# A two-layer graph network on one core: ScalarE's queue reordered, gate sums in two buffers, filter matrices loaded one by one

## The chip, the cores and the metric

One core of one Trainium2 chip. The time is the device time of one execution in microseconds; each kernel is executed several times, on the same chip in turn with the kernel before, and the median is quoted. A ratio is the mean time of one kernel's fast runs over the mean of the other's fast runs of the same rounds, so it is not quite the ratio of the medians quoted beside it. A profile adds one traced execution; its span is about 2 us shorter than the device time.

Engines are named as in the profile: PE is TensorE (PEld its weight loads), DVE VectorE, ACT ScalarE, POOL GpSimd, SP SyncE, which issues most transfers (415 of the 514 in the profile of the kernel before).

## The reference, cut to what matters

For 64 graphs ("items") of 256 nodes with 256 features, in float32:

```python
# layer 0
h      = relu(bn1(conv1x1(x^T)))
x_conv = relu(bn2(conv17(h)) + x^T)^T                  # 17 taps along the nodes
s      = x @ w_se.T + b_se                             # 3 numbers per node
A      = exp(-dist(s, s)) * adj
x_nmp  = A @ relu(x @ w_msg.T + b_msg)
gi     = [x_conv, x_nmp] @ w_ih.T + b_ih;  gh = x @ w_hh.T + b_hh
r, z   = sigmoid(gi_r + gh_r), sigmoid(gi_z + gh_z)
n      = tanh(gi_n + r * gh_n)
x      = layernorm(x + (1 - z) * n + z * x)
# layer 1
h      = layernorm(x)
x      = layernorm(x + relu(adj @ h @ W_rel + b_rel + h @ W_root))
```

## The kernel before

The gates of one item are three sources (`nmp`, `x`, `xc`) times a 2 x 2 block matrix. The kernel uses a Strassen-like scheme with seven block products instead of eight; "U5" is the product with index 4, which goes into the bank `b_`, is copied to `g11`, and whose bank is then used again by the product with index 2. All matmul outputs of this kernel rotate through eight PSUM banks (`bufs=8`), so a bank that was not read in time holds up whichever matmul comes eight banks later (in the kernel before, ps_b waited 85.5 us in all for the copy of U5).

```python
def gates(k):
    g = work.tile([P, C, 2, HG], F32, name="g", bufs=1)
    ...
    block_product(k, 0, a, True);   nc.scalar.copy(g00, a[:, :HG])
    block_product(k, 1, d, True);   ve.tensor_add(g00, g00, d[:, :HG])
    nc.gpsimd.tensor_add(g00, g00, bg[:, 1, :])
    yield
    block_product(k, 4, b_, True);  nc.scalar.copy(g11, b_[:, :HG])      # the copy of U5, L710
    block_product(k, 6, c_, True);  ve.tensor_add(g11, g11, c_[:, :HG])
    yield
    block_product(k, 5, a, False)
    ve.tensor_add(<g01 and g10>, <a twice>, bg)
    nc.gpsimd.tensor_add(g11, g11, g01)
    yield
    block_product(k, 2, b_, False); ve.tensor_add(g01, g01, b_[:, :HG])   # needs the bank b_ read
    nc.scalar.activation(<tanh of g0>)
    yield
    block_product(k, 3, c_, False); ve.tensor_add(g10, g10, c_[:, :HG])
    nc.scalar.activation(<tanh of g1>)
    yield

def update(k):                     # last part of three: layer norm of the item
    ...                            # VectorE: bn_stats; GpSimd: add, pow, mul, scale -> sh, q
    for i, dst in ((1, H[k]), (0, w)):
        for n in range(C):         # h and x1: four ScalarE instructions, L774
            nc.scalar.activation(dst[:, n, :], w[:, n, :], AF.Identity, bias=sh[...], scale=q[...])

def factors(k):                    # transposes st into a bank, ScalarE copies it out twice (lr)
    ...
def aggregate(k):                  # y: four steps; the third is Square on ScalarE, then GpSimd
    ...                            # (scale, pow, mul), the fourth the last Identity on ScalarE
```

In these traces an engine's instructions stand in the order in which the program emits them (moving one emitted step by four lines moved the copy of U5 ahead of h and x1 in 63 of 64 items, see order_only). The program software-pipelines three to four items; the order within the loop over items is therefore the schedule:

```python
for k in range(b * BG, (b + 1) * BG):
    ga, up = gates(k), update(k)
    load(k + 3)
    step(ga)                        # products 0, 1
    step(y_left)                    # y of item k - 2, second step
    step(up_left)                   # h and x1 of item k - 1
    pump()                          # a share of the next block's convolution
    step(ga)                        # products 4 (U5), 6
    mask(k + 1)
    step(y_left)                    # y, third step (Square)
    pump()
    step(ga)                        # product 5
    step(y_left)                    # y, fourth step (waits for GpSimd)
    pump()
    factors(k + 2)                  # lr: two ScalarE copies
    step(ga)                        # product 2
    ...
    transposes_h(k - 1); messages(k + 3); pump()
    passing(k + 1); sums(k + 1, "x")
    step(ga)                        # product 3
    ...
```

`pump()` emits the convolution of the next block of eight items, which is done by an FFT-like transform on VectorE with products on TensorE. It is paced by a fixed estimate of both engines' times, so the mix of VectorE work is decided when the program is built.

## Time and profile before

| | before |
|---|---|
| median time | 2394.8 us (3 runs) |
| TensorE busy | 2173.5 of 2392.4 us |
| VectorE busy | 1869.8 us |
| granted TensorE clock, mean | 0.962 |
| TensorE's waits in all (sum of that view) | 210.3 us |

Read it as two engines near their limit that wait for one another: 219 us of TensorE and 523 us of VectorE are idle. Most of VectorE's idle time lies where it has no transform to do; the stretches in the prediction show the part where both are nearly full. The lines of this profile stand in the prediction.

### The profile page before, as it was taken

The numbers are of one execution on the slowest core, as the hardware profiler recorded it, in microseconds if no ns is written. First come the engines' busy times: TensorE is split into PE (matmuls) and PEld (weight loads), VectorE is DVE, ScalarE is ACT, GpSimd is POOL, SyncE is SP. The second block draws the span as 40 slices with busy tenths as digits, with TensorE's granted clock in tenths as the row PEclk, the third lists the DMA queues.
The fourth block names the chain that finished last, engine by engine and source line by source line (L and its number), as shares of the span: only waits on it lengthen the run. The fifth ranks groups of instructions, "written<-read, shape, count | busy, mean of one in ns | idle before, by whom it ended". The sixth has DMA issues, their size and how long they took to land. (4 is left out here: it accounts for less than half of the span.)

```text
span 2392.4 us, 26243 instructions
## 1 busy us (share of the span) xinstructions
PE 2173.5 (91%) x8390; PEld 1508.2 (63%) x8390; DVE 1869.8 (78%) x4172; ACT 946.0 (40%) x2065; POOL 506.9 (21%) x744
## 2 busy tenths in 40 slices
PE   7878898898989999899988999889998999989996
PEld 4555576665766666666666667666676666766664
DVE  3895899758986699948988489875898669996563
ACT  4414332453235442354323533245323544235443
POOL 1002221222122231122212132122212223112221
PEclk9989999999989999999999999999999999999998
DMA  5533152221522234131432215222152222411110
GB/s 158 183 133 115 31 172 84 84 84 56 173 75 95 69 102 148 55 110 49 139 117 71 97 38 171 85 87 84 53 177 71 94 71 97 153 56 58 45 36 18
DMA packets 213942, 226.80 MB, mean 95 GB/s; under 512 B 22327, under 2 KB 205614, under 8 KB 213806
## 3 DMA queue, kind: packets, MB, share of 16 engines
q1 hardware_dynamic: 191248, 191.14, 24.8%
q10 hardware_dynamic: 22558, 33.99, 3.8%
q8 instruction: 68, 1.11, 0.2%
q14 instruction: 68, 0.56, 0.1%
HBM read 179.22 MB, written 45.88 MB: 94 GB/s over the span
## 5 line engine op out<-in xcount | busy, mean ns | idle before, releaser
L106 DVE SCALAR_TENSOR_TENSOR XF<-XF 128x512 f32<-128x512 f32 (+2 forms) x800 | 521.9, 688 | 6.8
L106 DVE TENSOR_TENSOR XF<-XF 128x256 f32<-128x256 f32 (+3 forms) x480 | 357.5, 764 | 43.9 <-ACT XF L494 36.3
L106 PE MATMUL ps_k<-w,XF 128*128 128x256 f32 x1316 | 295.1, 380 | 2.9 <-DVE msg L106 1.5
L106 PEld LDWEIGHTS ps_k<-w,XF 128*128 128x128 f32 x1316 | 250.8, 191 | 51.4 <-issue 4.3
L106 PE MATMUL ps_out<-wrr,hT 128*128 128x512 f32 x512 | 232.2, 596 | 4.6 <-ACT hT L788 4.6
L106 PE MATMUL ps_b<-wg,nmpsum 128*128 128x384 f32 x256 | 115.5, 535 | 107.7 <-ACT g L710 85.5
L764 POOL TENSOR_TENSOR q<-mv,eps 128x4 f32<-128x4 f32 x64 | 12.9, 202 | 917.8 <-DVE mv L106 917.8
L106 PEld LDWEIGHTS ps_out<-wrr,hT 128*128 128x128 f32 x512 | 97.4, 192 | 103.4 <-issue 89.2
L106 PE MATMUL ps_nmp<-AT,msg 128*128 128x256 f32 x512 | 130.5, 400 | 25.2 <-DVE g L106 22.5
L774 ACT ACTIVATE h<-x,sh,q 128x256 f32<-128x256 f32 x128 | 69.8, 593 | 200.9 <-POOL sh L768 200.9
L631 POOL TENSOR_SCALAR st<-ns 128x4 f32<-128x4 f32 x64 | 25.4, 397 | 580.8 <-DVE sq L106 357.8
L106 DVE TENSOR_TENSOR g<-g,ps_c 128x384 f32<-128x384 f32 x128 | 70.4, 550 | 90.6 <-ACT g L710 63.9
L106 PE MATMUL ps_msg<-wms,xT 128*128 128x260 f32 x512 | 127.8, 393 | 3.9 <-DMA adj<-in_adjT_dram 3.5
L106 PEld LDWEIGHTS ps_b<-wg,nmpsum 128*128 128x128 f32 x256 | 44.2, 198 | 137.6 <-ACT g L710 93.6
L106 PE MATMUL ps_out<-hr,adj 128*128 128x256 f32 x512 | 128.1, 392 | 1.0 <-ACT hr L800 0.9
L106 PEld LDWEIGHTS ps_nmp<-AT,msg 128*128 128x128 f32 x512 | 99.8, 199 | 43.4 <-DVE g L106 25.4
L106 PE MATMUL ps_c<-xTc,w 128*128 128x512 f32 x256 | 118.2, 604 | 8.6 <-ACT xTc L483 8.6
L718 POOL TENSOR_TENSOR g<-g 128x384 f32<-128x384 f32 x64 | 84.5, 1320 | 183.9 <-DVE g L106 183.2
L106 DVE TENSOR_TENSOR msg<-ps_msg,bmsg 128x256 f32<-128x256 f32 x128 | 52.5, 416 | 88.7 <-PE ps_nmp L106 88.7
L106 PE MATMUL ps_n<-wn,xT 128*128 128x256 f32 x512 | 120.9, 379 | 0.0
L106 PE MATMUL ps_c<-wg,nmp 128*128 128x384 f32 x256 | 110.0, 513 | 9.1 <-DVE y L106 9.1
L831 ACT ACTIVATE y<-y,sh,v 128x256 f32<-128x256 f32 x128 | 69.9, 593 | 121.1 <-POOL sh L828 118.3
(144 smaller groups left out, 4442.3 us busy)
## 6 DMA issues: line engine op xcount, KB each, us to landing
w<-w2m SPq DMA_DIRECT2D x105, 768.0 KB, 5.0
xn<-in_x_dram SPq DMA_DIRECT2D x32, 512.0 KB, 4.3
xt<-xTc ACTq DMA_DIRECT2D x32, 512.0 KB, 4.8
xT<-xt SPq DMA_DIRECT2D x64, 256.0 KB, 3.0
adj<-in_adjT_dram SPq DMA_DIRECT2D x64, 256.0 KB, 3.7
x<-in_x_dram SPq DMA_DIRECT2D x64, 256.0 KB, 2.7
xb<-in_x_dram SPq DMA_DIRECT2D x32, 512.0 KB, 3.5
out_dram<-y ACTq DMA_DIRECT2D x64, 256.0 KB, 2.2
```

The costliest lines, as they stand in the source:

```text
L106: return op(o, *args, **kwargs)
L631: nc.gpsimd.tensor_scalar(twice[:, :, :, 3], ns.unsqueeze(2).to_broadcast([P, C, 2]), 0.5, None, ALU.mult)
L718: nc.gpsimd.tensor_add(g11, g11, g01)
L764: nc.gpsimd.tensor_tensor(q, mv[:, :, 1].unsqueeze(1).to_broadcast([P, 2, C]), eps2, ALU.add)
L774: nc.scalar.activation(dst[:, n, :], w[:, n, :], AF.Identity, bias=sh[:, i, n:n + 1], scale=q[:, i, n:n + 1])
L831: nc.scalar.activation(y[:, n, :], y[:, n, :], AF.Identity, bias=sh[:, n:n + 1], scale=var[:, n:n + 1])
```

## The change

Its intent: ScalarE is idle most of the time but is waited for, because ready copies stand behind steps that wait for GpSimd. So the copy of U5 goes ahead of h and x1; the relu of the messages, which waits for VectorE, goes to a later place; g gets a second buffer, so that the first copy of an item need not wait for the last reader of the item before; the sum of g11 is rearranged; the block of the messages (nmp) is multiplied last and its sums are made earlier. The memory for the second g comes from loading the filters one matrix at a time (14 KB in place of 18 KB per partition) and from a single AT.

```diff
 def load_w(b, first, n):
-    t = work.tile([P, 3, C, D], F32, tag="w2", name="w2", bufs=3)
-    nc.sync.dma_start(out=t[:, :n], in_=w2m[first:first + n].rearrange("f c p o -> p f c o"))
-    return lambda m, c: t[:, m, c, :]
+    ts = [work.tile([P, C, D], F32, tag="w2", name="w2", bufs=7) for _ in range(n)]
+    for m, t in enumerate(ts):
+        nc.sync.dma_start(out=t, in_=w2m[first + m].rearrange("c p o -> p c o"))
+    return lambda m, c: ts[m][:, c, :]
 ...
-        nc.scalar.activation(MSG[k], MSG[k], AF.Relu)          # in messages(k)
+    def rectify(k):
+        nc.scalar.activation(MSG[k], MSG[k], AF.Relu)
 ...
-        AT[k] = work.tile([P, C, N], F32, tag="AT", name="AT")
+        AT[k] = work.tile([P, C, N], F32, tag="AT", name="AT", bufs=1)
 ...
-        for j, (name, w) in enumerate((("nmp", ...), ("x", ...), ("xc", ...))):
+        sources = [("xc", ...), ("x", ...), ("nmp", ...)]
+        for j, (name, w) in enumerate(sources if k % BG else sources[::-1]):
 ...
-        g = work.tile([P, C, 2, HG], F32, name="g", bufs=1)
+        g = work.tile([P, C, 2, HG], F32, name="g")            # two buffers
 ...
-        nc.gpsimd.tensor_add(g11, g11, g01)
+        ve.tensor_add(g11, g11, a[:, :HG])
+        nc.gpsimd.tensor_add(g11, g11, bg[:, 0, :])
 ...                                                            # the loop over items
             step(y_left)
-            step(up_left)
             pump()
             step(ga)
             mask(k + 1)
+            step(up_left)
             step(y_left)
 ...
+            sums(k + 1, "x"); sums(k + 1, "xc")                # before passing, not after
             pump()
             passing(k + 1)
 ...
             project(k - 1)
+            sums(k + 1, "nmp")                                 # was after distances
             step(up)
             pump()
             distances(k + 2)
+            rectify(k + 3)
```

(Guards for the last items, and the start before the first item, are cut.)

More of the change, by code (lines that the diff above doesn't have):

```diff
@@ L689, in block_product @@
     def block_product(k, i, ps, start):
-        for j, (name, w) in enumerate((("nmp", wg[:, i, 1, :]), ("x", wx[:, i, :]), ("xc", wg[:, i, 0, :]))):
+        sources = [("xc", wg[:, i, 0, :]), ("x", wx[:, i, :]), ("nmp", wg[:, i, 1, :])]
+        for j, (name, w) in enumerate(sources if k % BG else sources[::-1]):
             te.matmul(ps[:, :w.shape[-1]], LEFT[k, name][i], w, start=start and j == 0, stop=j == 2,
-                             skip_group_check=not start)
+                      skip_group_check=not start)
     def gates(k):
-        g = work.tile([P, C, 2, HG], F32, name="g", bufs=1)
+        g = work.tile([P, C, 2, HG], F32, name="g")
         G[k] = g
@@ L925, in weight_sums @@
                 nc.gpsimd.tensor_sub(w[:, i], w[:, j], w[:, l])
-    early = [lambda: messages(0), lambda: messages(1), lambda: factors(0), lambda: distances(0), lambda: mask(0),
-             lambda: factors(1), lambda: distances(1), lambda: passing(0), lambda: messages(2),
+    early = [lambda: messages(0), lambda: rectify(0), lambda: messages(1), lambda: rectify(1), lambda: factors(0), lambda: distances(0), lambda: mask(0),
+             lambda: factors(1), lambda: distances(1), lambda: passing(0), lambda: messages(2), lambda: rectify(2),
              lambda: sums(0, "x"), lambda: weight_sums((6, 2, 4), (4, 4, 0)), lambda: sums(0, "nmp"),
@@ L976, in gnn_two_layers @@
                 messages(k + 3)
+            if k + 1 < B:
+                sums(k + 1, "x")
+                if (k + 1) % BG:
+                    sums(k + 1, "xc")
             pump()
@@ L979, in gnn_two_layers @@
                 passing(k + 1)
-                sums(k + 1, "x")
             step(ga)
@@ L985, in gnn_two_layers @@
                 project(k - 1)
-            if k + 1 < B and (k + 1) % BG:
-                sums(k + 1, "xc")
+            if k + 1 < B:
+                sums(k + 1, "nmp")
             step(up)
@@ L991, in gnn_two_layers @@
                 distances(k + 2)
-            if k + 1 < B:
-                sums(k + 1, "nmp")
+            if k + 3 < B:
+                rectify(k + 3)
             pump()
```

## The prediction

> **What bounds the kernel now.** I read the page's busy line first, then the busy time in stretches of 14 us, then the waits of TensorE and VectorE, then one stalled item in the timeline. The busy line says TensorE is the busiest engine:
>
> ```profile
> PE 2173.5 (91%) x8390; PEld 1508.2 (63%) x8390; DVE 1869.8 (78%) x4172; ACT 946.0 (40%) x2065; POOL 506.9 (21%) x744
> ```
>
> 2392.4 - 2173.5 = 219 us of TensorE is idle. By 100 us stretches, 52 of it lies in the first 200 us (filters are built, the change does not touch them) and 18 in the last 92; about 149 us lie in the 2100 us between. There the 64 items run in eight blocks of eight, and beside each block but the last VectorE carries the transform of the next block's convolution. The stretches show what that means (columns: the stretch, its length, busy us and count of PE, PEld, DVE, ACT, POOL, then granted clock, DMA share, GB/s):
>
> ```profile
> 1276.00:1290.00 14.00, 10.70 (x40) 7.75 (x39) 11.98 (x29) 7.47 (x18) 6.85 (x10) 0.88 0.21 75
> 1290.00:1304.00 14.00, 14.00 (x51) 8.82 (x50) 13.72 (x32) 3.72 (x9) 0.17 (x1) 1.00 0.28 96
> 1304.00:1318.00 14.00, 10.97 (x44) 8.18 (x43) 8.41 (x17) 8.41 (x18) 6.85 (x10) 0.76 0.27 93
> ```
>
> The first two together are one item: TensorE has 24.7 us of work, VectorE 25.7. Both are nearly full, and both lose about 3 us at the same place. Over a whole transform stretch (1080 to 1318 us) TensorE is busy 217.7 of 238 us and VectorE 210.9. So the kernel has two bounds of almost equal size, and the idle time comes from their waiting for one another and for a third. The waits name the third:
>
> ```profile
> PE ps_b L106 <- ACT g L710: 85.5, 29, 4.1
> PE ps_nmp L106 <- DVE g L106: 22.5, 7, 3.7
> PE ps_b L106 <- DVE nmpsum L106: 22.1, 14, 2.7
> ```
>
> ```profile
> DVE g L106 <- ACT g L710: 63.9, 30, 4.0
> ...
> DVE g L106 <- POOL g L718: 34.4, 34, 1.3
> ...
> DVE XF L106 <- ACT XF L435: 30.2, 21, 3.0
> ```
>
> L710 is ScalarE's copy of the fifth gate product (U5) out of its bank. ScalarE is only 40% busy, so it is late because of its order and not its load. One case:
>
> ```profile
> 1306.42 0.22 POOL L768 TENSOR_SCALAR sh<-sh 128x4 f32<-128x4 f32 x1
> ...
> 1306.68 1.09 ACT L774 ACTIVATE h<-x,sh,q 128x256 f32<-128x256 f32 x2 [3.54 <-POOL sh L768]
> ...
> 1307.67 1.08 ACT L774 ACTIVATE x<-x,sh,q 128x256 f32<-128x256 f32 x2
> 1308.65 0.46 ACT L710 COPY g<-ps_b 128x384 f32<-128x384 f32 x1
> ...
> 1309.14 0.56 DVE L106 TENSOR_TENSOR g<-g,ps_c 128x384 f32<-128x384 f32 x1 [2.86 <-ACT g L710]
> 1309.16 0.50 PEld L106 LDWEIGHTS ps_b<-wg,nmpsum 128*128 128x128 f32 x2 [3.31 <-ACT g L710]
> 1309.16 1.65 PE L106 MATMUL ps_b<-wg,nmpsum 128*128 128x384 f32 x2 [3.03 <-ACT g L710]
> ```
>
> The bank was ready about 1302; the copy stood behind h and x1 of the item before, which stood behind four GpSimd steps of the statistics. One further wait holds the head of that queue:
>
> ```profile
> ACT g L702 <- DVE x L106: 115.1, 35, 8.2
> ```
>
> L702 writes the only buffer of g, which VectorE still reads for the item before.
>
> [...] a ready 0.46 us copy waited for two groups it does not need. [...] Here a 3.03 us wait was followed by a pair of matmuls in 1.65 us that takes 0.81 elsewhere, with a granted clock of 0.76 in that stretch; the 2.84 us wait at 555 us was followed by 0.91. So some stalls cost more than their length. [...]
>
> **The change part by part.**
> Reordering ScalarE: h and x1 (4 x 0.59 us and the wait for the statistics) go behind the copy of U5. The order of the built program confirms it: the sums' two copies now stand next to one another, then h and x1. This removes L710 as a cause: 85.5 us on TensorE, 63.9 us on VectorE. Since VectorE is the tighter one in those items (13.72 of 14 in the second half), I count its 63.9 us and not the 85.5. In the products stages a copy of a filter product (L435) stood behind h and x1 too: at 1231 us VectorE waited 2.97 us for it. Once per block, 7 x 2.9, gives 20 us of the 30.2.
> Two buffers of g: takes away the 115.1 us of L702. By itself this is ScalarE's idle time; it lets L710 come early, so it is in the 63.9 already.
> The sum g11: GpSimd's add of g01 becomes a VectorE add from the bank, 64 x 0.55 us (the row of the same shape from PSUM) = 35.2 us more VectorE work. It removes VectorE's wait for GpSimd before it overwrites g01, 34.4 us. Net +1.
> Order of sums and sources: the nmp block is multiplied last in seven items of eight, so its sums have 1.4 us more (0.81 and 0.59 us of matmuls), and its sums stand earlier on VectorE. That attacks 22.1 us on TensorE; where VectorE is the bound it only moves the wait. I count 5.
> Relu of messages later: its 173.2 us of ScalarE waiting (L629) no longer holds the copy of nmp behind it. Its reader comes two items later. Counted in the 5.
> Filters one by one: 7 buffers of 2 KB per partition in place of 3 of 6, with AT in one buffer (-2 KB): this pays for the second g (+6 KB). It makes 112 transfers into 329 of 256 KB. No TensorE wait for them is in the waits of before; seven matrices lead by one group of six (5.3 us of matmuls) plus the 3.5 us of other work between groups, against some 3 us to land. I count 0.
> Sum: 63.9 + 20 - 1 + 5 = 88 us. As items shorten, other waits grow (VectorE for the messages' product, 88.7 us today; TensorE for VectorE). I take off a quarter: 66 us, so 2394.8 - 66 = 2329 us, 2.8% less.
>
> **The rivals.**
> VectorE takes the place of ScalarE. For: 13.72 of 14 us in the half item after a stall, and 35 us of new work. Against: it idles 27 us of those 238 itself. If only a third of the gain survives, 2394.8 - 30 = 2365.
> TensorE is freed fully. If all of the 149 us but VectorE's share went: a transform stretch can't go under 218 of 238 us, 20 us seven times, 2255. The slow clock after stalls speaks for a part of it; two engines in fixed orders at 91 and 90% speak against the whole.
> A transfer or the later h takes over. The filters' lead falls from nine matrices to seven and SyncE waits 457 us for buffers already. h is wanted by the transposes one gate product after its new place; if they waited 1 us in 64 items, +64 us and the gain is gone. In the trace h is done by 1307.8 where its transposes start at 1314, so moving it 0.5 to 2 us is safe there.
>
> **Range and chances.** The 88 us undiscounted and some better clock give 2298; a discount of 60% gives 2362. The 2% line lies at 2347, 48 us down. My middle of 66 lies 18 us beyond it, with a spread of about 28 us: faster 0.73, within 2% 0.26, slower 0.01.
>
> **What would show it.** Right: the wait of ps_b for L710 (renumbered) falls from 85.5 us to under 10, VectorE's for it likewise; ScalarE's copy of ps_a no longer waits for VectorE's x; VectorE's busy time grows by about 35 us to 1905; the granted clock rises above 0.962; transform stretches show VectorE near 95%. What TensorE then waits for is VectorE. Wrong: a wait of ps_hT for h, or of ps_k for w, of more than 20 us in all; or VectorE idle staying near 11% in the transform stretches, which would mean the orders of the two engines and not ScalarE set the loss.

## The result, and the profile after

| | before | after |
|---|---|---|
| median time | 2394.9 us (4 runs) | 2339.5 us (4 runs) |
| ratio | 1 | 0.9765, 95% interval 0.9748 to 0.9782 |
| TensorE busy | 2173.5 us | 2150.9 us |
| VectorE busy | 1869.8 us | 1910.9 us |
| TensorE's waits in all | 210.3 us | 175.8 us |
| granted clock | 0.962 | 0.975 |

The changed kernel is 2.35% faster. Its span fell by 56.0 us, from 2392.4 to 2336.4. On TensorE that is 33.4 us less idle time (218.9 to 185.5) and 22.6 us less busy time for the same 8390 matmuls: the mean granted clock was 0.975 against 0.962, and the 256 matmuls of the sums of nmp in ps_b (128x384) took 486 ns on average against 535. On VectorE it is 97 us less idle time, against 41 us more busy time.

The busy line of the page after the change:

```profile
PE 2150.9 (92%) x8390; PEld 1484.7 (64%) x8390; DVE 1910.9 (82%) x4236; ACT 938.8 (40%) x2065; POOL 477.1 (20%) x744
```

TensorE's waits after the change (who waited, for whom: us in total, times, longest):

```profile
PE ps_hT L106 <- ACT h L780: 34.9, 31, 5.0
PE ps_nmp L106 <- ACT lr L644: 31.3, 7, 4.5
...
PE ps_k L106 <- DVE y L106: 15.3, 7, 2.2
PE ps_n L106 <- ACT lr L644: 12.9, 13, 1.2
...
PE ps_k L106 <- ACT lr L644: 6.6, 14, 0.5
...
PE ps_dist L106 <- ACT lr L644: 5.7, 2, 4.6
```

The three lines of before (85.5, 22.5 and 22.1 us) are gone; none of them appears at all. (order_only below shows that the last two go with other parts of the change than the order.) In their place stand the transposes of h waiting for h (5.0 us of it is a single wait that was there before, too), and four different matmuls waiting for lr, 56.5 us in all. Both new lines name ScalarE again.

VectorE's waits after the change:

```profile
DVE msg L106 <- PE ps_nmp L106: 104.8, 20, 7.1
DVE g L106 <- PE ps_c L106: 39.2, 24, 2.2
...
DVE XF L106 <- ACT XF L436: 8.8, 14, 0.6
```

The wait for the copy of U5 (63.9 us) and the one for GpSimd's sum (34.4 us) are gone, and the one for the copies of the filter products fell from 30.2 to 8.8 us. What VectorE waits for now is TensorE.

VectorE's busy time grew by 41 us, but not by the new add alone. The groups of instructions by shape show a second row, first before, then after (count, then busy us, mean ns of one, idle us before it):

```profile
L106 DVE TENSOR_TENSOR AT<-AT,adj 128x512 f32<-128x512 f32 x64 | 43.8, 684 | 0.0
```
```profile
L106 DVE TENSOR_TENSOR AT<-AT,adj 128x512 f32<-128x512 f32 x64 | 56.9, 888 | 0.0
```

This is the mask, a multiplication with both inputs in SBUF. 28 of the 64 take up to 1.50 us where before none took over 0.69, and each of the 28 overlaps GpSimd's add of bg to g, which none of the other 36 does. It comes with the order: order_only has 21 long ones, u_order none. The 64 new adds, with one input in PSUM, take 0.54 to 0.55 us each, 34.8 us in all.

The first new cause, in one item, from the timeline after (start, length, engine, line, what; in brackets the idle time before it and what ended it):

```profile
966.57 0.39 DVE L106 BATCH_NORM_STATS2 bst<-x 128x6 f32<-128x256 f32 x1
967.00 0.18 DVE L106 BATCH_NORM_AGGREGATE mv<-bst 128x2 f32<-128x6 f32 x1
...
967.54 1.04 POOL L771 TENSOR_TENSOR q<-q,mhalf 128x4 f32<-128x4 f32 x1
...
969.12 0.56 POOL L774 TENSOR_SCALAR sh<-sh 128x4 f32<-128x4 f32 x1
...
969.71 1.09 ACT L780 ACTIVATE h<-x,sh,q 128x256 f32<-128x256 f32 x2 [6.04 <-POOL sh L774]
...
970.36 0.33 PE L106 MATMUL ps_hT<-ident,h 128*128 128x128 f32 x1 [3.10 <-ACT h L780]
```

ScalarE was free for 6.04 us and started h 0.03 us after its input was there. The input comes from four GpSimd steps, which took 2.53 us after VectorE's last statistic. So here ScalarE is only the last link, though the line of the waits names it. The trace shows the same for all 31 waits: ScalarE had been idle for 4.2 us or more and took h as soon as GpSimd was done, and in 30 of them VectorE had been 94 to 96% busy in the 8 us before its last statistic. So VectorE came late to the statistics; how much of the wait is due to GpSimd's 2.5 us was not tested. The stretch that begins there agrees (stretch, length, then busy us and count of PE, PEld, DVE, ACT, POOL, clock, DMA share, GB/s):

```profile
970.00:998.00 28.00, 27.24 (x99) 18.39 (x100) 27.52 (x64) 12.64 (x29) 9.08 (x13) 0.94 0.28 85
```

VectorE is busy 98% of it. It was 25.7 of 28 us in the item that the prediction shows of before. Over nearly the whole of a transform stretch (1070 to 1280 us after, against 1080 to 1318 us before) it is 97% against 89%. TensorE's 27.24 us contain slower matmuls after the 3.10 us wait: the eight of ps_msg at 971.24 us took 2.84 us, those at 720.63 us 1.92, and the granted clock was 0.75 from 970.3 to 973.8 us.

The second new cause is of another kind. ScalarE's timeline after:

```profile
722.15 0.49 ACT L830 ACTIVATE hr<-y,sum 128x256 f32<-128x256 f32 x1
722.55 0.19 ACT L830 ACTIVATION_READ_ACCUMULATOR hr<-y,sum 128x1 f32 x1
725.68 1.09 ACT L837 ACTIVATE y<-y,sh,v 128x256 f32<-128x256 f32 x2 [2.94 <-POOL sh L834]
726.80 0.38 ACTq L838 DMA_DIRECT2D out_dram<-y  x1
727.23 0.56 ACT L643 ACTIVATE lr<-ps_sT,lone 36x256 f32<-36x256 f32 x1 [0.46 <-ACT y L837]
727.69 0.35 ACT L644 COPY lr<-ps_sT 36x256 f32<-36x256 f32 x1
...
728.10 3.78 PE L106 MATMUL ps_nmp<-AT,msg 128*128 128x256 f32 x8 [4.47 <-ACT lr L644]
...
731.92 0.42 DVE L106 TENSOR_TENSOR msg<-ps_msg,bmsg 128x256 f32<-128x256 f32 x1 [6.25 <-PE ps_nmp L106]
```

The bank that lr is copied from had been written by 717.4 (two transposes, 0.38 us together). Its copies stood behind the last step of y, which waited 2.94 us for GpSimd. The product that needed the bank eight places later waited 4.47 us, and then ran in 3.78 us, at a granted clock of 0.50, where the same group takes 1.89 in lr_early below. VectorE waited 6.25 us for that product. This is the very pattern that the change removed for the copy of U5. Before the change lr stood in the same place and cost TensorE 4.9 us in all, presumably because TensorE came later itself.

### The profile page after: what moved, and what is told of

Same layout as the page of the kernel before. It is cut to its first block, busy times and chain, and to the rows that moved or that the text cites.

```text
span 2336.4 us, 26606 instructions
## 1 busy us (share of the span) xinstructions
PE 2150.9 (92%) x8390; PEld 1484.7 (64%) x8390; DVE 1910.9 (82%) x4236; ACT 938.8 (40%) x2065; POOL 477.1 (20%) x744
## 5 line engine op out<-in xcount | busy, mean ns | idle before, releaser
L106 PE MATMUL ps_k<-w,XF 128*128 128x256 f32 x1316 | 302.0, 382 | 38.3 <-DVE y L106 15.3
L106 PE MATMUL ps_nmp<-AT,msg 128*128 128x256 f32 x512 | 135.7, 412 | 31.3 <-ACT lr L644 31.3
L106 DVE TENSOR_TENSOR msg<-ps_msg,bmsg 128x256 f32<-128x256 f32 x128 | 52.4, 415 | 104.8 <-PE ps_nmp L106 104.8
L733 ACT ACTIVATE g<-g 128x512 f32<-128x512 f32 x64 | 40.4, 631 | 236.3 <-DVE g L106 236.2
L631 POOL TENSOR_SCALAR st<-ns 128x4 f32<-128x4 f32 x64 | 15.3, 240 | 553.5 <-DVE sq L106 316.3
L757 ACT ACTIVATE gn<-gn 128x512 f32<-128x512 f32 x64 | 40.4, 631 | 212.6 <-DVE gn L106 212.6
L106 PEld LDWEIGHTS ps_n<-wn,xT 128*128 128x128 f32 x512 | 96.2, 190 | 44.3 <-ACT lr L644 22.3
L106 PEld LDWEIGHTS ps_out<-hr,adj 128*128 128x128 f32 x512 | 92.0, 189 | 31.2 <-ACT hr L806 17.6
L106 PE MATMUL ps_c<-wg,xc 128*128 128x384 f32 x256 | 107.9, 504 | 0.0
```

The source lines that it names most:

```text
L106: return op(o, *args, **kwargs)
L631: nc.gpsimd.tensor_scalar(twice[:, :, :, 3], ns.unsqueeze(2).to_broadcast([P, C, 2]), 0.5, None, ALU.mult)
L733: nc.scalar.activation(g[:, 1, :, :2 * P], g[:, 1, :, :2 * P], AF.Tanh, scale=0.5)
L757: nc.scalar.activation(nn, nn, AF.Tanh)
```

## The experiments

Beside the changed kernel twelve more ran, each with three timed rounds beside the kernel before. "The order" means the move of h and x1 behind the copy of U5 and nothing else. All results were correct except the one that is wrong on purpose.

| run | what it is | median us | ratio to before |
|---|---|---|---|
| after | the changed kernel | 2339.5 | 0.9765 |
| u_order | after, the order undone | 2366.4 | 0.9872 |
| order_only | before, the order alone | 2340.8 | 0.9765 |
| g_one_buffer | after, g in one buffer | 2340.3 | 0.9764 |
| g11_on_gpsimd | after, old sum of g11 | 2330.9 | 0.9729 |
| vector_plus | after, 35 us more VectorE work | 2360.3 | 0.9853 |
| vector_minus | after, 35 us less (wrong result) | 2319.8 | 0.9685 |
| stream_only | before, filters one by one | 2398.1 | 1.0011 |
| sources_back | after, nmp multiplied first | 2339.6 | 0.9760 |
| relu_back | after, relu at its old place | 2339.5 | 0.9761 |
| lr_early | after, lr ahead of y's last step | 2293.4 | 0.9574 |
| order_and_lr | before, the order and lr early | 2323.7 | 0.9694 |
| lr_early_gpsimd | lr_early, old sum of g11 | 2300.2 | 0.9594 |

The half-width of the 95% interval of each ratio is 0.0014 to 0.0019, some 3 to 5 us; a difference of two is uncertain by some 5 to 6 us.

### u_order and order_only: is it the order?

The edit is the same one line moved, in u_order backwards from the changed kernel, in order_only alone on the kernel before:

```diff
             step(y_left)
-            step(up_left)
             pump()
             step(ga)
             mask(k + 1)
+            step(up_left)
             step(y_left)
```

In both, only ScalarE's order differs from the kernel that was edited; the other engines' orders were compared and are the same.

> The changed kernel with one part undone: h and x1 stand ahead of the copy of U5 on ScalarE again. The orders of TensorE, VectorE, GpSimd and SyncE stay those of the changed kernel, and g keeps two buffers. Theory (ScalarE's order made the gain): 2375 to 2395 us, and TensorE waits 60 us or more for the copy of U5 again. Rival (the nmp block multiplied last, earlier sums and two buffers made the gain): 2335 to 2350 us, under 25 us of that wait.

> The kernel before with one part alone: h and x1 behind the copy of U5; one buffer of g, filters in threes, GpSimd's add and the old orders stay. Theory (ScalarE's order made the gain, the buffer only helps): 2335 to 2360 us, the wait for the copy of U5 under 25 us. Rival (the copy can't come early while g has one buffer, because the first copy of the item waits for VectorE's last read of g): 2375 to 2395 us, with 50 us or more of that wait left.

Measured: the order alone gives 2340.8 us, the whole gain of the change. Without it, all other parts together give 2366.4 us, 1.3%: between the two figures, so a mixture, though its wait is just as the theory said. From the waits of u_order:

```profile
PE ps_b L106 <- ACT g L715: 92.3, 29, 6.7
```

and from those of order_only:

```profile
PE ps_b L106 <- DVE nmpsum L106: 31.4, 21, 2.6
PE ps_xc L106 <- ACT lr L641: 22.7, 7, 3.2
PE ps_nmp L106 <- DVE g L106: 19.5, 7, 2.8
```

In order_only the copy of U5 has left the list although g has one buffer. What remains there are the waits for the sums of nmp and for VectorE's adds to g, which the other parts of the change remove, and the new wait for lr. So the two sets of parts take 56 and 30 us off alone and 55 together: they do not add. For the same reason the order is worth 56 us on the kernel before, but 27 us from u_order to the changed kernel, though there it takes away 92.3 us of TensorE's waiting. Something else limits the sum. The next runs look for it.

### g_one_buffer: is the second buffer needed?

```diff
-        g = work.tile([P, C, 2, HG], F32, name="g")
+        g = work.tile([P, C, 2, HG], F32, name="g", bufs=1)
```

> The changed kernel with g in one buffer again and every order unchanged. Theory (the buffer's own share is small, as VectorE reads g last some 3 us before TensorE needs the bank): 2339 to 2355 us, the wait of ps_b for ScalarE under 20 us. Rival (the two buffers are needed for the gain): 2365 us or more.

Measured: 2340.3 us, ratio 0.9764 against 0.9765. The buffer is worth nothing that these runs resolve. Its profile is instructive all the same:

```profile
PE ps_a L106 <- ACT g L707: 16.8, 7, 2.4
...
PE ps_hT L106 <- ACT h L780: 12.0, 18, 5.0
```

The wait for h fell from 34.9 to 12.0 us, a new one of 16.8 us appeared for the first copy, and the time did not move. A wait can thus move to another instruction without changing the time.

### g11_on_gpsimd, vector_plus, vector_minus: what is VectorE's time worth?

g11_on_gpsimd takes the old sum back. The estimate that paces the convolution is charged as if the VectorE add were still there, so that all other instructions keep their order:

```diff
-        ve.tensor_add(g11, g11, a[:, :HG])
-        nc.gpsimd.tensor_add(g11, g11, bg[:, 0, :])
+        clock.vector("tensor_add", HG)
+        nc.gpsimd.tensor_add(g11, g11, g01)
```

vector_plus writes g01 a second time with the same value, 0.55 us in each item; vector_minus leaves the new VectorE add out and puts nothing in its place:

```diff
+        nc.vector.tensor_add(g01, a[:, :HG], bg[:, 0, :])      # vector_plus
```
```diff
-        ve.tensor_add(g11, g11, a[:, :HG])                     # vector_minus
+        clock.vector("tensor_add", HG)
```

> The changed kernel with g11 += g01 on GpSimd again, as before, and VectorE without the extra 35 us of adds; the orders of the rest are the same. If the two cancel, as the prediction counts: 2335 to 2345 us, and VectorE waits some 34 us for GpSimd. If VectorE is the bound of what is left and the add costs its whole time: 2315 to 2330 us. If GpSimd's add was the worse one: 2350 us or more.

> The changed kernel with one VectorE add of 0.55 us more in each item (the same value is written into g01 twice, so the result stays right), all orders else unchanged: 64 x 0.55 = 35 us more VectorE work. Theory (VectorE is the bound of about half of the items of the changed kernel, and the wait of ps_hT for h is VectorE in disguise): 12 to 25 us slower than the changed kernel of 2340 us. Rival (ScalarE's order or TensorE sets those items too): 0 to 6 us slower.

> The changed kernel without VectorE's add of the fifth product's bank to g11, 35 us of VectorE work less and nothing put in its place; the result is wrong on purpose. Theory (VectorE is the bound in about half of the items): 2318 to 2330 us, at most as fast as the version with the add on GpSimd (2331 us) or some us faster, as no wait for GpSimd replaces it. Rival (not VectorE): 2335 to 2341 us.

Measured: the added add (35.7 us of instructions) cost 20.8 us (2360.3 - 2339.5), the one left out (34.8 us) gained 19.7 us; both theories were met. VectorE's busy time as a whole changed by 38.4 and by 29.1 us, as other instructions took longer or shorter with it. So 0.54 to 0.68 of a VectorE microsecond, spread over all items, is on the path that sets the end. This is an average and does not count items. The lengths of the items, from one ScalarE copy of ps_a to the next (means of blocks 2 to 7), show a little more: with the added work six of the eight items of a block grow by 0.6 us each, which is the whole add, the first by 0.1, and the last gets 0.5 us shorter; with less work they gain from 0 to 1.0 us.

The wait for h is 39.0 us in vector_plus and 28.9 us in vector_minus, with ScalarE's order the same. It does not follow VectorE's work alone: it is 33.7 us in g11_on_gpsimd, where VectorE is busy 48 us less, and 26.1 us in relu_back, where only ScalarE's order differs.

The old sum is better than the new one by 8.6 us (0.9729 against 0.9765, intervals 0.9712 to 0.9747 and 0.9748 to 0.9782), which lies between the figures for "cancel" and for "costs its whole time". VectorE then waits for GpSimd again:

```profile
DVE g L106 <- POOL g L724: 72.9, 57, 2.1
```

This is twice the 34.4 us of before, and still cheaper than the add: VectorE's busy time is 48 us lower. What the wait costs can be read from vector_minus, which has the same VectorE instructions and no such wait: it is 11.0 us faster. So 72.9 us of waiting cost some 11 us. Part of the 72.9 us must lie where VectorE would have waited for TensorE otherwise; its wait of msg for TensorE is 78.9 us here against 104.8.

### stream_only: do the filters' transfers matter?

The edit is the first part of the diff above, alone on the kernel before.

> The kernel before with only the filters' loads changed: matrices one by one into seven buffers of their own, in place of threes in three buffers. If this part only frees memory: within 4 us of the kernel before, no wait of ps_k for w. Rival (it takes part in the gain, as smaller transfers land sooner, or harms, as it leads by seven matrices and not nine): more than 8 us either way.

Measured: 2398.1 us, 3.1 above the kernel before; ratio 1.0011, interval 0.9996 to 1.0026. No wait of ps_k for w appears. A matrix of 256 KB took 3.6 us to land (median), three in one transfer of 768 KB 5.0 in the kernel before. The part is only a source of memory. That it is one was seen in building: the kernel before with two buffers of g does not build, not even with a single AT (the build's message: 131.9 KB wanted per partition, 128.0 left).

### sources_back and relu_back: the order of sources and the relu

```diff
-        for j, (name, w) in enumerate(sources if k % BG else sources[::-1]):   # sources_back
+        for j, (name, w) in enumerate(sources[::-1]):
```
```diff
                 messages(k + 3)                                                # relu_back
+                rectify(k + 3)
 ...
-                rectify(k + 3)                                                 # from behind distances
```

> The changed kernel with the nmp block multiplied first again in every item; only TensorE's order moves. The prediction counted some 5 us for this part with the earlier sums: 2342 to 2352 us, with a wait of ps_a or ps_b for the sums of nmp of 10 us or more. Rival (where VectorE is the bound it only moves the wait): 2337 to 2342 us.

> The changed kernel with the relu of the messages back behind the messages, ahead of the copy of nmp on ScalarE. The prediction gave it nearly nothing: 2338 to 2344 us. Rival (the relu holds the copy of nmp and through it the sums and the banks): 2350 us or more, with a wait of TensorE for the copy or the sums of nmp of 15 us or more.

Measured: 2339.6 and 2339.5 us. So for sources_back the rival's figure was met, for relu_back the prediction's. Neither part is worth anything in the changed kernel, each undone alone. In sources_back no wait for the sums of nmp came back, so their earlier place on VectorE seems to be enough; it was not undone alone.

### lr_early: the same trick once more

Only ScalarE's order changes: the two copies of lr go ahead of y's last step.

```diff
             step(ga)
-            step(y_left)
             pump()
             factors(k + 2)
+            step(y_left)
             step(ga)
```

> The changed kernel with ScalarE's two copies of the factors (lr) ahead of the last step of y, which waits for four GpSimd steps; nothing else moves. Aim: the waits of ps_nmp (31.3), ps_n (12.9), ps_k (6.6) and ps_dist (5.7 us) for lr. Theory (a copy stands behind a waiting step once more; where TensorE sets the items its waits count in full, but the half in VectorE's items comes back as another wait): 2310 to 2332 us. Rival (all items are VectorE's, TensorE's waits for ScalarE are worth nothing): 2336 to 2342 us.

Measured: 2293.4 us, 46 us less than the changed kernel and more than I expected; ratio 0.9574 to the kernel before. TensorE's waits in it begin:

```profile
PE ps_hT L106 <- ACT h L780: 31.8, 23, 5.0
PE ps_tT L106 <- DVE ws L106: 17.1, 13, 2.5
PE ps_k L106 <- DVE y L106: 15.3, 7, 2.2
```

Of the 56.5 us of waits for lr, the 5.7 us of ps_dist and 2.6 us of ps_xc are left. VectorE's wait of msg for TensorE fell from 104.8 to 64.9 us. TensorE's wait for lr had lain just before the product with the messages, which VectorE waits for (the 6.25 us in the timeline after), so both engines stood still for the same reason, as they had with the copy of U5 before. The lengths of the items show where the 46 us lie: the last item of a block took 29.1 us before, 33.5 us in the changed kernel and 26.9 us in lr_early, and no other one differs by more than 0.6 us between the last two. So the change itself had made that item 4.4 us longer. The wait for h stayed at 31.8 us.

### order_and_lr and lr_early_gpsimd: do the pieces add?

order_and_lr is the kernel before with the two moves on ScalarE's queue, two lines moved, and nothing else of the change. lr_early_gpsimd is lr_early with the edit of g11_on_gpsimd.

> The kernel before with two moves on ScalarE's queue and nothing else: h and x1 behind the copy of U5, the factors' copies (lr) ahead of the last step of y. If the other parts of the change are worth nothing even without the lr waits: 2290 to 2300 us, as fast as the changed kernel with lr early (2293 us). If they are worth something once the lr waits are gone: 2305 to 2325 us. The order alone was 2341 us, its waits for lr 36 us.

> The changed kernel with lr early and with g11 += g01 on GpSimd again, to beat both kernels: the two gains were 46 and 9 us alone. If they add, as the VectorE dose suggests: 2280 to 2288 us. If the wait for GpSimd comes to stand in the way once lr is early: 2290 to 2297 us.

Measured: order_and_lr 2323.7 us, 30 us slower than lr_early. So the other parts, which were worth nothing beside the order (0.9765 both), are worth 1.2% once the wait for lr is gone; that wait had hidden them. Its own profile has the wait of ps_b for the sums of nmp at 33.2 us and of ps_nmp for VectorE's adds at 19.7 us. Which of the parts pays was not taken apart.

lr_early_gpsimd came to 2300.2 us, ratio 0.9594 (interval 0.9580 to 0.9608) against 0.9574 (0.9560 to 0.9588) of lr_early: the 9 us of the old sum are not there a second time, and neither of my two figures was met. VectorE's wait for GpSimd is 71.6 us in it. By its median lr_early is the best version; its interval overlaps that of lr_early_gpsimd.

## Why the prediction was right, and where its sum was off

The prediction said 2329 us, in a range of 2298 to 2362; measured were 2339.5. Direction, mechanism and class held; that the sum came so close is luck in part, as shown below. Step by step, in the order of its parts:

- **Reordering ScalarE.** The claim was that TensorE and VectorE wait for the copy of U5 only because of its place in the queue. order_only shows it: the move alone removes the wait and gives 56 us. 56 us lies nearer to VectorE's 63.9 than to TensorE's 85.5, but no run separates the two counts, and the gain is net of new waits (36 us for lr in order_only). Of the waits for the copies of the filter products, counted as 20 us, 21.4 went away (30.2 to 8.8); what that is worth in time was not measured apart.
- **Two buffers of g.** Counted as nothing of its own; measured nothing (g_one_buffer).
- **The sum g11.** This term was mis-sized. "Net +1" set 35.2 us of adds against 34.4 us of wait, each at full size. The adds took 34.8 us, as counted, each of them 0.54 to 0.55 us, also the 36 that ran while GpSimd was busy. But undoing the part gains 8.6 us: the adds are worth 19.7 us of time, the wait of 72.9 us only 11.0. The mistake is to set a microsecond of work against a microsecond of waiting: the waiting lay partly in places where VectorE would have waited for TensorE anyway. VectorE's busy time grew by 41.1 us and not by 35 chiefly because of the mask, which under the new order overlaps GpSimd's add (13 us more) and which the prediction did not foresee.
- **Order of sums and sources, relu.** 5 us counted, nothing measured by undoing the sources or the relu alone. The reason given ("where VectorE is the bound it only moves the wait") may not be the whole one: the wait for lr hid 1.2% that belongs to some of the parts other than the order.
- **Filters one by one.** 0 counted, 0 measured (stream_only). The "some 3 us to land" were an estimate of mine from the profile of before (2.7 us for 256 KB of x, 5.0 for 768 KB of filters); measured were 3.6 us, and 3.7 in the changed kernel.
- **The deduction of a quarter.** By VectorE's own books: waits removed 63.9 + 34.4 + 21.4 = 119.7 us, more work 41.1, left 78.6; the span fell by 56.0, so other waits grew by 22.6 us. The prediction took off 22. The size agrees, and 16.1 of the 22.6 are the wait for the messages' product that the prediction named (88.7 to 104.8). But a quarter was a flat guess, and it stood for a loss that was not foreseen, the last item of each block made longer by lr; that the two agree is luck. The 10 us between forecast and result are the 5 of the sums and the 6 by which VectorE's busy time grew more than counted.

The rivals. The first (VectorE takes ScalarE's place) came true in part: 0.54 to 0.68 of VectorE's time counts (vector_plus, vector_minus), and it is busy 97% of a transform stretch. The third asked whether the transposes of h would come to wait for h and called the move safe, as h was done at 1307.8 and wanted at 1314.4. They do wait now, 34.9 us in all, where over 20 us was the prediction's own sign of being wrong. It read h's slack from an item in which TensorE had just lost 3 us to the stall that the change removes. The move itself did not delay h, as ScalarE was idle before h in all 31 waits: it was h's input that came late. With 23 us of the wait moved elsewhere (g_one_buffer) the time stays. No rival named lr, the largest loss that the change uncovered, though the timeline of before had the same pattern in it.

What the prediction said would show it: the wait for U5 under 10 us (gone); VectorE busy 1905 (1910.9); clock above 0.962 (0.975); ScalarE's copy of ps_a no longer waiting for VectorE's x (gone); VectorE near 95% in transform stretches (97% from 1070 to 1280 us). One sign failed: "what TensorE then waits for is VectorE" does not hold for lr, and for h only through GpSimd.

Three slips of the recorded text change nothing in its sum: a discount of 60% gives 2360 and not 2362; VectorE's 210.9 of 238 us are 89% and not 90; and between h's new place and its transposes stand two gate products (5 and 2), not one.

What stays open: which of the sums, the sources, the relu and the buffer bring the 30 us in the absence of the order, and the 30 us once lr is early (the sum g11 gave 7 us of these in lr_early against lr_early_gpsimd, not clear of the noise); and what GpSimd's steps add to the wait for h.

## What to carry to other kernels

When an idle engine is waited for, look at what stands ahead of the late instruction in its queue: a copy that frees a PSUM bank belongs ahead of every step that waits for another engine. Here two such moves on an engine that is 40% busy were worth 56 and 46 us of 2395. After one such move look at once for the next in the same queue, for a wait that was harmless while everything was late can hide gains from other parts (lr here: 4.9 us before, 56.5 us after). When two engines are nearly full, count what the tighter one loses and measure with a small dose of extra work on it what its microsecond is worth, before paying for anything with its time. After a reordering compare the mean lengths of the instructions, too: those that newly overlap can have become longer, as the mask did here (684 to 888 ns).

## How matmuls ran after two waits

In the kernel before, TensorE waited 2.17 us before 1223.31 us, and a pair of matmuls that takes 0.81 us elsewhere then took 1.62; the granted clock was 0.57 from 1223 to 1227 us. The longer wait of 2.84 us before 555.13 us was followed by such a pair in 0.91 us, with a granted clock of 1.00 from 555 to 559 us. So the length of a wait alone did not decide it; what did was not shown. Timeline of before:

```profile
1220.33 0.81 PE L106 MATMUL ps_d<-wg,xc 128*128 128x384 f32 x2
1223.31 1.62 PE L106 MATMUL ps_b<-wg,nmpsum 128*128 128x384 f32 x2 [2.17 <-DVE nmpsum L106]
```
